# A new order for all pieces of a hand-ordered graph kernel, with one product step cut in two

## Chip, cores and metric

The kernel runs on one core of a Trainium2 chip. The metric is device microseconds (us) of one execution. Times inside an execution come from one profiled run and are counted from the first instruction. TensorE is PE in the profile (PEld is its weight load), VectorE is DVE, ScalarE is ACT, GpSimd is POOL, and SP issues the DMAs.

## What is computed

There are 128 graphs of 128 nodes with 64 features. Layer 0 sums, over each node's neighbours, the positive part of a sum of two projections, and multiplies by a second weight. Layer 1 is a small message pass with a gated update. Each layer ends with a residual and a layer norm.

```python
mask = adj > 0                                            # layer 0
diff = x[:, :, None, :] - x[:, None, :, :]
h = relu((x @ W1a)[:, :, None, :] + diff @ W1b + b1)      # 192 hidden columns
x = layernorm(x + einsum('bjkh,bjk->bjh', h, mask) @ W2 + deg[..., None] * b2)

m = relu(relu(x @ W1 + b1) @ W2 + b2)                     # layer 1
msg = relu(adj @ m)
r, z, n = gates(msg @ W_ih.T + b_ih, x @ W_hh.T + b_hh)
x = layernorm(x + (1 - z) * n + z * x)
```

## The kernel before

The graphs are taken in 32 groups of four. The sparse sum of layer 0 is done with gathers: a 0/1 matrix (`pick0`, `pick1`) picks neighbour rows on TensorE, its product lands in a PSUM tile `pv` that ScalarE has seeded (`seed0`, `seed1`), and ScalarE (`keep`, L656) or VectorE (`reduce`, `reduce1`, L666) takes the positive part and adds it up. There are 24 gather steps of 12 products in a group (L636).

Each group's work is a set of Python generators, one for each kind of piece; each `yield` ends a step, and nearly each step holds the instructions of one engine. The order is written out by hand: `TIMETABLE` gives every step of a kind a number, in units of which 100000 (`PER`) lie between one group and the next. Group g's step is put at g x 100000 plus its number, all steps are sorted, and the program is issued in that order. The numbers are used for nothing else. Every engine works through its own instructions strictly in the order that comes out. `FIRST` replaces the numbers of some kinds for the first group and `SETUP` places the steps of the set-up. The steps of up to six groups lie within one period.

Below, `sums0.1` is the second step (counted from 0) of the kind `sums0`. The steps that the text speaks of:

- `pieces`: step 0 projects x (L547, PE). Steps 1, 2, 5, 6, 9, 10 are ScalarE copies to bf16 (L574) of the two halves; steps 3, 4, 7, 8 subtract each copy in PSUM with one product of 384 columns (L577, PE).
- `sums0`, `sums2`: the turned sums. Step 0 is three transposes (L711, PE). Step 1 is two products of all 128 columns (L718) and two products of 64 columns (L723), four weight loads each because they are float32. The last step copies them to SBUF (L729, ACT).
- `second`: step 0 and 1 are products (L284, L288, PE), step 2 adds a residual and takes the statistics (L292, L254, L256, DVE), step 3 is three tiny GpSimd operations (`ve` L259, `nm` L261, `rs` L263), step 4 one more (L265, `nm` times `rs`), step 5 is four ScalarE operations that write x1 (L269). `turn.0` (L299, PE) transposes x1.
- `update`: step 0 is a tanh (ACT, L361), steps 1 to 4 are GpSimd (L364, L367, L370, L373), step 5 the second statistics (L254, L256, DVE), step 6 `ve`, `nm`, `rs` and step 7 their product on GpSimd, step 8 writes the output (ACT).
- `pick0` (L518 twice, L532 twice) and `pick1` (L518, L540): VectorE compares and subtracts bf16 tiles that all lie in SBUF.
- `offsets`: products (L455), two small copies (L458, L460, ACT), step 2 is four GpSimd operations (L466, `till`), step 3 a product (L469), step 4 two copies (L472, L474).
- GpSimd also has `masks` (L415), `counts`, `others` (L479, L481), `together0` to `together3` (three steps each: L686, L688, L691) and `joined0`, `joined2` (L699). ScalarE also has `base0` to `base3` (L678), `turned.1` (L490), `owners.1` (L498).

PSUM gives three tiles to `pv` and two to everything else, in turn.

Of the kernel before, what the change touches and what calls it, by code (L numbers as in the profile page):

```python
# [28 lines left out]

PER = 100000  # L30
TIMETABLE = {
    "load": (-268618,), "masks": (-266066,), "ranks": (-232900, -232900), "degrees": (-257102, -254423),
    "turned": (-224742, -220574), "counts": (-234901,), "offsets": (-217678, -211964, -197704, -192380, -189932),
    "owners": (-35894, -35894), "places": (-179586, -177714),
    "pieces": (-221915, -212465, -212465, -212025, -212025, -210034, -207896, -206287, -204509, -201502, -201502),
    "others": (-93885, -63613), "values0": (-168677, -168312, -168312), "pick0": (-187243, -177588, -157318, -147219),
    "pick1": (-101562, -99096), "over0": (-86465, -86465), "over2": (-91716, -89070), "base0": (-71690,),
    "base1": (-115079,), "base2": (-74898,), "base3": (-66289,), "together0": (-90368, -86071, -54801),
    "sums0": (-16639, -16639, -6895), "joined0": (-42043,), "joined2": (-9054,),
    "together1": (-31159, -22707, -22707), "together2": (-54332, -29252, -26680), "sums2": (-10324, -7550, -6743),  # L40
    "together3": (-14410, -11697, -11388), "second": (1322, 1729, 6614, 12070, 12714, 14947), "turn": (17589, 19125),
    "message1": (22148, 22871), "message2": (24221, 25357), "message3": (34134, 47496),
    "gates": (52002, 52335, 59212, 59212, 60471, 61641),
    "update": (63484, 134926, 134926, 146356, 147450, 212137, 231447, 236648, 276814),
    "seed0": (-137838, -111380, -107532, -90909, -89996, -88760, -70167, -48540),
    "gather0": (-132826, -123102, -109699, -102053, -101463, -95122, -90696, -82750, -82750, -77811, -77618, -69952,
        -66122, -48012, -38905, -32104), "keep0": (-129922, -97944, -81962, -65602),
    "reduce": (-116740, -102949, -100299, -89511, -89215, -81357, -75312, -71801, -69013, -44762, -33692, -24596),
    "seed1": (-80653, -43141), "gather1": (-77673, -72671, -67801, -55447, -41338, -33923, -28108, -20295),
    "keep1": (-76545, -38998), "reduce1": (-70927, -59829, -52180, -31003, -23063, -16037),  # L50
}


SETUP = (-227883, -212853, -185033, -155144, -101231, 22249)
FIRST = {
    "load": (-236749, -176840), "masks": (-192323,), "ranks": (-160512, -153527), "degrees": (-172354, -159518),
    "turned": (-108605, -102394), "counts": (-146837,), "offsets": (-115482, -109556, -106790, -103472, -99536),
    "places": (-98687, -93949),
    "pieces": (-169807, -166786, -164278, -164278, -164278, -164278, -158634, -152826, -143767, -142875, -113691),
    "values0": (-148521, -139633, -130220), "pick0": (-141784, -133982, -133982, -103074), "pick1": (-92485, -74065),  # L60
    "over0": (-88306, -87641),
}


# [1 line left out]
def adj_resnorm_kernel(  # L66
# [166 lines left out]
    def made(s, key, pool, shape, dtype, **how):  # L233

        if key not in s:
            s[key] = pool.tile(shape, dtype, **how)
        return s[key]
# [146 lines left out]
    with ExitStack() as fast:  # L384
# [259 lines left out]
        def kept(s, t, i):  # L644
            if t:
                return s["acc1", i]
            return s["acc0", i // 2][:, i % 2]
# [56 lines left out]
        def sums(s, i0):  # L704

            def part():
                g, q = s["g"], i0 // 2
                p = ps_w.tile([N, 3, N], F32, tag="w", name=f"ph{g}")
                fs = s["fs", q].rearrange("p b h -> p (b h)")
                for i, c in ((0, 0), (1, 2), (2, 1)):  # L710
                    nc.tensor.matmul(  # L711
                        p[:, i, :], fs[:, c * N : (c + 1) * N], ident, start=i == 0, stop=False, is_transpose=True,
                        skip_group_check=True,
                    )
                yield
                a = kept(s, 1, q)
                for i in range(2):
                    nc.tensor.matmul(  # L718
                        p[:, i, :], a[:, 0, i, i * F : i * F + N], s["ownT"][:, i0 + i, :], start=False, stop=True,
                        skip_group_check=True,  # L720
                    )
                for i in range(2):
                    nc.tensor.matmul(  # L723
                        p[i * F : (i + 1) * F, 2, :], a[:, 0, i, (1 - i) * N : (1 - i) * N + F], s["ownT"][:, i0 + i, :],
                        start=False, stop=True, skip_group_check=True,
                    )
                yield
                hmT = made(s, "hmT", main, [N, 2, 3, N], F32, tag="hmT", name=f"hmT{g}", bufs=2)
                nc.scalar.copy(hmT[:, q], p)  # L729

            return part
# [14 lines left out]
        name, g, run = "setup", -1, setup(ps_g, ps_w)  # L746
        for t in SETUP:
            plan.setdefault(t, []).append(run)
# [143 lines left out]
```

## Time and profile before

| | us |
|---|---|
| median of three runs | 966.61 (966.36 to 968.12) |
| the profiled execution, whole | 966.97 |
| its span, first to last instruction | 965.2 |
| start of the first gather of group 0 | 18.18 |
| of group 2 | 85.73 |
| of group 31 | 906.70 |
| from there to the end | 58.50 |

The span is 1.8 us shorter than the execution. The first two periods take 31.76 and 35.79 us; from group 2 on a period takes 28.29 us nearly without change. The granted clock is 0.98 over the span: the trace has it at 0.5 from 19.4 to 43.3 and from 84.2 to 91.1, and at 1.0 in between and after, up to the end of the program. PE is busy for 907.4 us, DVE 827.3, ACT 841.4, POOL 840.7.

### The profile page before, as it was taken

To read this page: it belongs to the slowest core of one execution; us is meant where nothing else is said; L and a number is where in the kernel's file an instruction comes from. 1 tells how busy PE (TensorE), PEld (TensorE's weight loads), DVE (VectorE), ACT (ScalarE), POOL (GpSimd) and SP (SyncE) were. 2 spreads that over 40 slices of the span, in tenths; PEclk is the share of its full clock that TensorE was granted. 3 is DMA by queue.
4 is the path that set the end of the run, shared out by engine and by line. 5 is a ranking of instruction groups with operands and counts; after the bars stand their busy time and mean duration, and the time that the engine had idled before them with its cause. 6 is when DMAs were issued, how large, how long until landed. Compare 5 with 4: busy or idle time off the path is not lost.

```text
span 965.2 us, 32667 instructions
## 1 busy us (share of the span) xinstructions
PE 907.4 (94%) x13333; PEld 723.1 (75%) x13335; DVE 827.3 (86%) x1586; ACT 841.4 (87%) x1762; POOL 840.7 (87%) x1233
## 2 busy tenths in 40 slices
PE   6888999999999999999999999999999999999984
PEld 3567777777877777878777787777778777777762
DVE  5687898888899888889988888988888898888962
ACT  3787899999999999999999999999999999999863
POOL 4576899999999999999999999999999999999774
PEclk6898999999999999999999999999999999999998
DMA  3000001111100111110001111011101001010000
GB/s 97 24 3 23 24 2 29 30 29 30 29 18 13 30 30 29 30 30 10 22 29 30 30 30 29 2 30 30 30 29 29 25 7 30 29 30 8 7 7 19
DMA packets 25565, 23.91 MB, mean 25 GB/s; under 512 B 4156, under 2 KB 21314, under 8 KB 25410
## 3 DMA queue, kind: packets, MB, share of 16 engines
q1 hardware_dynamic: 25410, 21.78, 7.9%
q8 instruction: 106, 1.74, 0.8%
q14 instruction: 49, 0.40, 0.1%
HBM read 17.57 MB, written 4.19 MB: 23 GB/s over the span
## 4 chain that ended last, share of the span: by engine, by line
PE 68%; ACT 14%; DVE 13%; issue 3%; POOL 1%; DMA 0%; SPq 0%; ACTq 0%; DVEq 0%; POOLq 0%
PE pv L636 32%; DVE acc L666 7%; ACT x L269 4%; PE ph L718 3%; PE pw L284 3%; PE pv L577 3%; ACT pv L606 3%; DVE pick L532 3%; ACT us L623 2%; PE pv L547 2%; PE pu L547 2%; PE ph L723 2%; PE ph L711 2%; PE pm L307 2%; PE pa L327 2%
## 5 line engine op out<-in xcount | busy, mean ns | idle before, releaser
L666 DVE SCALAR_TENSOR_TENSOR acc<-pv,acc 128x768 f32<-128x768 f32 x576 | 534.4, 952 | 102.6 <-PE pv L636 90.4
L636 PE MATMUL pv<-b,pick 64*128 64x192 bf16 x9216 | 465.9, 245 | 21.0 <-DVE acc L666 17.0
L636 PEld LDWEIGHTS <-pick 64*128 64x128 bf16 x9216 | 379.2, 95 | 92.9 <-issue 69.9
L606 ACT COPY pv<-u 128x768 f32<-128x768 f32 x256 | 206.3, 816 | 1.1 <-DVE acc L666 1.0
L656 ACT ACTIVATE acc<-pv 128x768 f32<-128x768 f32 x192 | 155.9, 812 | 17.1 <-PE pv L636 16.9
L686 POOL TENSOR_TENSOR acc<-acc 128x384 f32<-128x384 f32 x128 | 143.7, 1123 | 12.9 <-DVE acc L666 12.9
L466 POOL TENSOR_SCALAR till<-iota,off 128x128 bf16<-128x128 bf16 x128 | 100.3, 801 | 7.8 <-ACT off L458 7.8
L574 ACT CAST b<-pv 128x384 bf16<-128x384 f32 x192 | 83.0, 486 | 19.7 <-PE pv L547 10.5
L691 POOL TENSOR_TENSOR fs<-acc,nb 128x192 f32<-128x192 f32 x128 | 75.9, 593 | 21.6 <-ACT nb L678 14.1
L699 POOL TENSOR_TENSOR acc<-acc 128x384 f32<-128x384 f32 x64 | 77.8, 1216 | 7.3 <-DVE acc L666 7.2
L688 POOL TENSOR_TENSOR acc<-acc 128x192 f32<-128x192 f32 x128 | 77.9, 608 | 2.6
L518 DVE TENSOR_TENSOR pick<-rankT,ramp 128x2048 bf16<-128x2048 bf16 x64 | 77.2, 1208 | 0.7 <-POOL npad L448 0.7
L606 ACT COPY pv<-us 128x768 f32<-128x768 f32 x64 | 51.4, 803 | 26.4 <-DVE acc L666 26.4
L259 POOL TENSOR_SCALAR ve<-mv 128x4 f32<-128x4 f32 x64 | 39.5, 617 | 35.5 <-DVE mv L256 35.4
L263 POOL TENSOR_TENSOR rs<-ve,nhalf 128x4 f32<-128x4 f32 x64 | 66.8, 1043 | 0.0
L415 POOL TENSOR_SCALAR maskT<-adjT 128x512 bf16<-128x512 f32 x32 | 61.2, 1912 | 6.1 <-DMA adjT<-in_adjT_dram 6.0
L617 PE MATMUL pz<-u,own 128*128 128x192 f32 x256 | 57.7, 348 | 0.9 <-ACT own L474 0.9
L678 ACT ACTIVATE nb<-u,npad 128x192 f32<-128x192 f32 x128 | 58.5, 458 | 0.0
L532 DVE TENSOR_TENSOR pick<-pick 128x1024 bf16<-128x1024 bf16 x64 | 50.4, 787 | 0.0
L269 ACT ACTIVATE x<-y,nm,rs 128x64 f32<-128x64 f32 x128 | 45.9, 432 | 4.8 <-POOL nm L265 4.8
L269 ACT ACTIVATE o<-y,nm,rs 128x64 f32<-128x64 f32 x128 | 45.9, 446 | 2.2 <-POOL nm L265 2.2
L617 PEld LDWEIGHTS pz<-u,own 128*128 128x128 f32 x256 | 39.8, 189 | 9.3 <-ACT own L474 5.9
(148 smaller groups left out, 1635.6 us busy)
## 6 DMA issues: line engine op xcount, KB each, us to landing
adjT<-in_adjT_dram SPq DMA_DIRECT2D x32, 256.0 KB, 3.0
xT<-in_xT_dram SPq DMA_DIRECT2D x64, 64.0 KB, 2.7
x<-in_x_dram SPq DMA_DIRECT2D x32, 128.0 KB, 2.3
out_dram<-o SPq DMA_DIRECT2D x32, 128.0 KB, 1.7
wab<-in_w_dram SPq DMA_DIRECT2D x2, 96.0 KB, 2.9
bi<-in_b_ih_dram SPq DMA_DIRECT2D x1, 96.0 KB
bias<-in_b_hh_dram SPq DMA_DIRECT2D x1, 96.0 KB
wx<-in_w_hhT_dram SPq DMA_DIRECT2D x2, 48.0 KB, 2.7
```

Of the source, the lines that this page charges most:

```text
L269: nc.scalar.activation(s[into][:, i, :], y[:, i, :], AF.Identity, bias=nm[:, i : i + 1], scale=rs[:, i : i + 1])
L466: nc.gpsimd.tensor_scalar(s["till"][:, i, :], iota, off[:, i : i + 1], None, ALU.is_lt)
L532: nc.vector.tensor_tensor(v[:, q, 1], v[:, q, 1], v[:, q, 0], ALU.subtract)
L574: nc.scalar.copy(b[c][:, h::2, :], ps[h])
L606: nc.scalar.copy(v, src.to_broadcast(list(v.shape)))
L617: nc.tensor.matmul(p[:, i, :], s["own32"][:, i0 + i, :], s["u"][:, i0 + i, :], start=True, stop=True)
L636: nc.tensor.matmul(v[:, h, j, :], pick[ks], s[f"b{c}"][ks, gr, :], start=False, stop=c == 2, skip_group_check=True,)
L656: nc.scalar.activation(kept(s, t, i), view(s["pv", t, i, 0]), AF.Relu)
L666: nc.vector.scalar_tensor_tensor(out=a, in0=view(s["pv", t, i, k // CH if t == 0 else 0]), scalar=0.0, in1=a, op0=ALU.max, op1=ALU.add,)
L686: nc.gpsimd.tensor_tensor(f[:, 0], f[:, 0], f[:, 1], ALU.add)
L688: nc.gpsimd.tensor_tensor(f[:, 0, 0], f[:, 0, 0], f[:, 0, 1], ALU.add)
L699: nc.gpsimd.tensor_tensor(f[:, 0], f[:, 0], f[:, 1], ALU.add)
```

## The change

One `yield` is added: the two products of 64 columns (L723) become a step of their own, `sums0.2` and `sums2.2`, and the copy to SBUF becomes step 3. All numbers of `TIMETABLE`, `SETUP` and `FIRST` are replaced. No instruction is added, removed or changed; the order in which the engines get them is.

```diff
-    "others": (-93885, -63613), "values0": (-168677, -168312, -168312), "pick0": (-187243, -177588, -157318, -147219),
+    "others": (-118434, -58619), "values0": (-174541, -170553, -168136),
...
-    "together0": (-90368, -86071, -54801),
-    "sums0": (-16639, -16639, -6895), "joined0": (-42043,), "joined2": (-9054,),
+    "together0": (-95088, -76907, -44507), "sums0": (-19812, -13451, -11960, -10058), "joined0": (-34125,),
+    "joined2": (-10568,),
...
-    "update": (63484, 134926, 134926, 146356, 147450, 212137, 231447, 236648, 276814),
+    "update": (62463, 117060, 142675, 149215, 150755, 189123, 200159, 250387, 280080),
...
                         p[:, i, :], a[:, 0, i, i * F : i * F + N], s["ownT"][:, i0 + i, :], start=False, stop=True,
                         skip_group_check=True,
                     )
+                yield
                 for i in range(2):
                     nc.tensor.matmul(
                         p[i * F : (i + 1) * F, 2, :], a[:, 0, i, (1 - i) * N : (1 - i) * N + F], s["ownT"][:, i0 + i, :],
```

Sorting both timetables gives the order on each engine. In a period of the steady part these stretches differ, and nothing else:

```text
PE    before  offsets.0 sums0.0 sums0.1(L718,L723) pieces.3 pieces.4 sums2.0 gather0.2 sums2.1(L718,L723) pieces.7 pieces.8 gather0.3
      after   offsets.0 sums0.0 sums0.1(L718) pieces.3 sums2.0 pieces.4 sums0.2(L723) gather0.2 pieces.7 sums2.1(L718) pieces.8 sums2.2(L723) gather0.3
DVE   before  reduce1.5 reduce.1 pick1.0 reduce.2 pick1.1 second.2 reduce.3 reduce.4 update.5 pick0.0
      after   reduce1.5 update.5 reduce.1 pick1.0 reduce.2 pick1.1 second.2 reduce.3 reduce.4 pick0.0
POOL  before  together3 joined2 offsets.2 others.0 together0.0 second.3 second.4 together0.1 update.6 masks update.1 update.2 others.1
              update.7 together0.2 together2.0 update.3 update.4 joined0 counts together1.0 together2.1 together2.2 together1.1 together1.2
      after   together3 others.0 joined2 offsets.2 update.6 together0.0 second.3 second.4 update.1 together0.1 masks others.1 update.2
              update.3 update.7 update.4 together0.2 together2 together1.0 counts together1.1 together1.2 joined0
ACT   before  update.0 owners.1 ... update.8 turned.1 base1 pieces.1 pieces.2 offsets.1 ... sums0.2 sums2.2 pieces.9 pieces.10
      after   owners.1 update.0 ... turned.1 update.8 pieces.1 offsets.1 pieces.2 ... sums0.3 pieces.9 sums2.3 pieces.10
      before  keep1.0 base2 message2.1 base0 seed0.6 values0.1 values0.2 base3
      after   base2 keep1.0 message2.1 seed0.6 base3 base1 values0.1 base0 values0.2
```

In the first periods, `ranks` of group 0 comes before its `pieces`, `pieces.8` before `values0.0`, and `offsets.0` to `offsets.3` of group 0 come earlier.

## The prediction

> **What bounds the kernel now.** I first read the busy shares and the chain that ended last, then the busy time of the steady part, then the timelines of POOL, DVE and PE's weight loads inside one period.
>
> ```profile
> PE 907.4 (94%) x13333; PEld 723.1 (75%) x13335; DVE 827.3 (86%) x1586; ACT 841.4 (87%) x1762; POOL 840.7 (87%) x1233
> ...
> PE 68%; ACT 14%; DVE 13%; issue 3%; POOL 1%; DMA 0%; SPq 0%; ACTq 0%; DVEq 0%; POOLq 0%
> ```
>
> PE is nearly full, but a third of the chain runs through other engines. The three stretches below (columns: stretch, its length, busy time of PE, PEld, DVE, ACT, POOL, clock, DMA share, GB/s) are the 29 periods from group 2 to group 31, what lies ahead of them, and what lies behind.
>
> ```profile
> 85.80:906.70 820.90, 802.15 (x12058) 645.62 (x12060) 734.83 (x1383) 754.44 (x1586) 761.29 (x1092) 1.00 0.08 24
> 0.00:85.80 85.80, 65.80 (x779) 48.28 (x782) 60.29 (x115) 55.28 (x107) 45.89 (x87) 0.82 0.15 41
> 906.70:965.20 58.50, 39.47 (x503) 29.23 (x500) 32.22 (x91) 31.63 (x71) 33.55 (x56) 0.93 0.04 14
> ```
>
> 820.9 / 29 = 28.3 us a period, so 0.1 us in each period is 2.9 us in the end. Where PE still waits inside a period is seen in its weight loads; the period shown starts at 396.97 (start, length, idle time before and what ended it):
>
> ```profile
> 400.99 0.53 PEld L718 LDWEIGHTS ph<-ownT,acc 128*128 128x128 f32 x4
> 401.63 0.20 PEld L723 LDWEIGHTS ph<-ownT,acc 128*64 128x64 f32 x4
> 402.00 0.11 PEld L577 LDWEIGHTS <-minus 128*128 128x128 bf16 x2 [0.17 <-issue]
> 402.18 0.41 PEld L711 LDWEIGHTS ph<-ident,fs 128*128 128x128 f32 x3
> ...
> 404.80 0.94 PEld L636 LDWEIGHTS <-pick 64*128 64x128 bf16 x24 [0.32 <-issue]
> ...
> 412.51 0.14 PEld L299 LDWEIGHTS pt<-ident,x 128*128 128x128 f32 x1 [0.31 <-ACT x L269]
> ```
>
> Wherever the shape of the weights changes (128*128, 128*64, 64*128), PE loses 0.1 to 0.3 us; between equal shapes (L577 to L711) next to nothing. The last line is the wait that matters most: `turn.0` waits for x1, the end of a chain through `second` on DVE, POOL and ACT. These are POOL and DVE there:
>
> ```profile
> 403.22 3.39 POOL L466 TENSOR_SCALAR till<-iota,off 128x128 bf16<-128x128 bf16 x4
> 406.58 1.27 POOL L479 TENSOR_TENSOR t<-b2bc,deg 128x256 f32<-128x256 f32 x1
> 407.82 0.99 POOL L686 TENSOR_TENSOR acc<-acc 128x384 f32<-128x384 f32 x1
> 409.07 0.23 POOL L259 TENSOR_SCALAR ve<-mv 128x4 f32<-128x4 f32 x1 [0.26 <-DVE mv L256]
> ...
> 410.70 0.20 POOL L265 TENSOR_TENSOR nm<-nm,rs 128x4 f32<-128x4 f32 x1
> ...
> 411.79 1.11 POOL L259 TENSOR_SCALAR ve<-mv 128x4 f32<-128x4 f32 x1 [0.35 <-DVE mv L256]
> ```
>
> ```profile
> 404.42 1.23 DVE L518 TENSOR_TENSOR pick<-place,ramp 128x2048 bf16<-128x2048 bf16 x1
> ...
> 406.44 0.94 DVE L540 TENSOR_TENSOR pick<-pick 128x1536 bf16<-128x1536 bf16 x1
> ...
> 408.90 2.02 DVE L666 SCALAR_TENSOR_TENSOR acc<-pv,acc 128x768 f32<-128x768 f32 x2
> 410.83 0.59 DVE L254 BATCH_NORM_STATS2 stats<-y 128x6 f32<-128x64 f32 x4
> 411.34 0.36 DVE L256 BATCH_NORM_AGGREGATE mv<-stats 128x2 f32<-128x6 f32 x4
> 411.62 1.19 DVE L518 TENSOR_TENSOR pick<-rankT,ramp 128x2048 bf16<-128x2048 bf16 x1
> ```
>
> Two rows of one operation tell the main thing: `ve` of `second.3` took 0.23 us, `ve` of `update.6` 1.11 us. The second was issued at 411.79, while the `pick` of 411.62 ran, and it ended at 412.90, just behind the pick's end at 412.81. A GpSimd operation issued during a pick on DVE stands until the pick is over, however small it is.
>
> **The change, part by part.** Nothing is added, so each engine's sum of work stays; what can change is waiting. Times below are on the shown period.
>
> *PE, turned sums.* From 400.71 to 404.80, 4.09 us, the loads themselves take 2.83 us and the gaps 1.26. After, the shape changes are: L577 to L723 twice, L723 to L636 twice, L636 to L577 once; the others are between equal shapes. L723 to the next is 0.17, L636 to a full array 0.16; L577 to another shape cost 0.32 behind two of the 384-column products, and I take 0.21 behind one. With 0.07 for L711 and L718 behind L577, the gaps are 2 x 0.21 + 2 x 0.17 + 0.16 + 2 x 0.07 = 1.06; the loads are 2.89: four single L577 of 0.10 for two pairs of 0.11, less 0.10 that L711 waited inside its 0.41 (0.31 in the first turned sum) and 0.02 of overlap. Sum 3.95: a gain of 0.14, say 0.15 us (0.35 if L577 to L723 cost nothing, a loss of 0.1 if each cost 0.32). The single products wait for ScalarE's copies: ACT loses `base1` here (0.47) but does `turned.1` first, which waits until PE's L487 are done at about 399.1, so `pieces.1` starts again near 400.8 and its copy is ready at 401.3, ahead of `pieces.3` near 401.5. `offsets.1` before `pieces.2` puts that at 401.8, ahead of `pieces.4` at 402.0. Cover of 0.2 each; without it PE would wait by what is missing.
>
> *DVE.* `update.5` (0.87 from 410.83 to 411.70) moves into the 1.81 us in which DVE waits ahead of `reduce.1` at 403.54; its input was written by POOL nine microseconds before. It costs nothing there, with 0.9 of cover. `pick0.0` then follows `reduce.4` directly, at 410.83 in place of 411.62, less the 0.15 that PE gained: **410.68 to 411.87**. `reduce.5` and `seed1.0` come earlier, which takes PE's wait for `seed1.0` (0.05 to 0.1, taken as 0.08).
>
> *POOL.* Now `update.6` (0.23 + 0.23 + 1.04 with its gaps: 1.55) stands ahead of `together0.0` and `second.3`, and `others.0` has left that place for one ahead of `joined2`. From the end of `reduce.11` at 399.14 POOL runs `together3` (1.01, 0.59, 0.59 and 0.15 between them) from 399.23 to 401.57 (before, it started at 399.94, behind other work), `others.0` to 402.14 (0.61 where no pick stands against it; the 1.27 shown holds a block), `joined2` to 403.10, `offsets.2` from 403.08. Its fourth operation meets `pick1.0` (404.42 to 405.65) and ends 0.46 behind that, at 406.1. `ve` and `nm` get through to 406.6; `rs` is due at 406.58, in `pick1.1` (406.44 to 407.38), and ends about 0.9 behind it, at 408.28 (blocked rows end their own length less 0.14 behind the pick: 412.90, and 406.58 + 1.27). `together0.0` ends at 409.2 and `second.3` starts at 409.2 (409.07 before; between 408.9, where the data would set it, and 409.4, if `nm` is blocked too). The distance from there to `second.4` is 410.70 - 409.07 = 1.63: due at **410.8**. That is inside the moved `pick0.0`.
>
> *What it costs.* `second.4` then ends behind the pick like the blocked `ve`, at 411.87 + 0.09 = 411.96 in place of 410.90. x1 started on ACT at 411.02, now at 412.05; `turn.0` at 413.54 for 412.51. That is 1.03 us of PE standing, and all of PE queues behind `turn.0`: `places`, `message1` and the gathers. The 0.15 gained ahead of it is lost in the same wait. From `turn.0` to the next `gather0.15`, which through `reduce.11` starts POOL's row again, the order on PE is unchanged, so only the 0.08 comes off: **+0.95 us a period** (0.85 to 1.1).
>
> *The rule.* The Trainium skill, "SBUF — State Buffer", section "SBUF: two separate sides", speaks against this move: a VectorE operation of that kind and a GpSimd one take a shared port pair as an exclusive lock for the whole instruction, and the other blocks. The rows agree on the side of GpSimd. By the page a GpSimd operation that came first would hold up DVE just as long; then `pick0.0` would start behind `rs`, and the loss would be some 0.1 us a period larger. The trace has a pick of 1.22 us at 413.60, begun while `rs` of 413.17 ran its 1.04, so I take no hold-up.
>
> *Everything else.* `masks`, `update.1` to `update.4`, `counts`, `joined0` and `base0` to `base3` feed nothing on PE for over 4 us; cover is lost only if POOL is over 0.7 us late at `together3`. SP issues the loads some 13 us ahead of `masks` (400.48 against 414.19), so moved loads and stores cost nothing. The head: before, `gather0.0` of group 0 waits for `pieces.8`, two copies and a seed until 18.18; with `values0.0` behind `pieces.8` I expect about 1 us less, and `offsets` of group 0 earlier perhaps 2 more, since POOL waits 7.8 us for it. I take -3 us (from -6 to +2, the 23.9 us at clock 0.5 there may move). Tail: no next `pick0.0` exists there, 0 +- 1.
>
> *Sum.* 966.97 + 29 x 0.95 - 3 = 991.5 for the profiled execution, which stood 0.36 above the median: **991 us**; with 0.85 to 1.1 and the head's bounds, 984 to 1001.
>
> **The rivals.** *POOL slips through (faster).* `second.4` is due only about 0.1 us inside the pick. If `rs` of `update.6` starts before `pick1.1` (0.14 earlier than I have it), `second.3` is set by its data, 0.15 earlier than before, and `second.4` ends before `pick0.0`. Then a period gains 0.15 + 0.08 = 0.23: 966.6 - 6.7 - 3 = 957. For: PE's switches are really fewer, and the blocks are decided by tenths. Against: `update.6` puts 1.55 us where 0.61 stood. It decides from `second.4` due before about 410.7.
>
> *One block only (about the same).* `rs` is blocked but `second.4` slips in: x1 is 0.13 late, 0.08 comes off, +0.05 a period: 966.6 + 1.5 - 3 = 965.
>
> *In turns.* `till` took 3.39 us in the shown period and 3.09 in others; if the block strikes in half of the periods, 966.6 + 14 - 3 = 977.
>
> *Worse.* POOL, late at `together3` too, holds up the sums: over 1001.
>
> **How the numbers follow.** Blocked in each period 0.55, slips through 0.20, one block 0.12, in turns 0.08, worse 0.05. The likeliest gives 991; its own range is 984 to 1001. To hold 8 in 10 the range must reach to the faster cases: 957 to 1001. A measurement of this kernel tells about 0.2% (1.9 us) from no change. Faster takes slipping through and part of one block: 0.25; same the most of one block: 0.07; slower the rest: 0.68.
>
> **What would show it.** In the changed profile: L265 at `second.4` at about 1 us in place of 0.20, once a period, and the wait of L299 for ACT `x` up from 0.3 to over 1 us; a period of 29.2 us; L577 standing alone with a gap of about 0.2 ahead of L723; no 1.81 us wait of DVE ahead of `reduce.1`. The prediction is wrong if L265 stays at 0.2 us, if the period falls below 28.3, or if L723 costs more behind L577 than 0.3 us.

## The result, and the profile after

The changed kernel takes 1002.57 us (median of 4 runs, 999.02 to 1006.38) against 967.07 for the kernel before (4 runs): a ratio of 1.036, 95% interval 1.034 to 1.038. Slower was forecast, at 991 with a range of 957 to 1001; the time lies 1.6 us above that range. The profiled execution took 999.02, the least of the four; its span is 997.2.

The three stretches of the changed profile, cut at the same pieces as before (first gather of group 2, first gather of group 31):

```profile
81.56:936.83 855.27, 803.11 (x12060) 646.57 (x12060) 739.07 (x1383) 757.46 (x1588) 761.63 (x1092) 0.99 0.08 23
0.00:81.56 81.56, 61.38 (x779) 45.73 (x780) 60.91 (x115) 54.66 (x106) 49.14 (x89) 0.90 0.16 43
936.83:997.16 60.33, 40.58 (x503) 29.88 (x500) 32.26 (x91) 31.61 (x71) 33.05 (x54) 0.90 0.04 13
```

The steady part grew by 34.4 us, the head shrank by 4.2 and the tail grew by 1.8; PE's busy time in the steady part is the same within 1 us (803.11 for 802.15), so nearly all of the time is waiting. An ordinary period takes 29.41 us for 28.29. (A correction to the section on the profile before: the two stretches at clock 0.5 given there are 11.4 us late. By the windows of that profile, 8.0 to 32.0 has 0.50 and 72.8 to 79.7 has 0.51; and the end, from 956.9 on, has 0.50 too, where that section says 1.0.)

The period shown from here on starts at 405.12. PE's weight loads in it (start, length, idle time before and what ended it; L724 is the L723 of the kernel before, one line further down for the added `yield`):

```profile
409.59 0.10 PEld L577 LDWEIGHTS <-minus 128*128 128x128 bf16 x1
409.99 0.41 PEld L711 LDWEIGHTS ph<-ident,fs 128*128 128x128 f32 x3 [0.29 <-issue]
410.36 0.10 PEld L577 LDWEIGHTS <-minus 128*128 128x128 bf16 x1
410.72 0.20 PEld L724 LDWEIGHTS ph<-ownT,acc 128*64 128x64 f32 x4 [0.26 <-issue]
...
421.06 0.14 PEld L299 LDWEIGHTS pt<-ident,x 128*128 128x128 f32 x1 [1.06 <-ACT x L269]
421.72 0.14 PEld L299 LDWEIGHTS pt<-ident,x 128*128 128x128 f32 x1 [0.53 <-ACT x L269]
```

The last two lines are the forecast wait: `turn.0` stands for x1, first 1.06 us and then 0.53, where before it was 0.31. The lines above them are a forecast that failed: behind a single L577 PE loses 0.29 and 0.26 us. GpSimd and VectorE in the same period:

```profile
414.83 0.95 POOL L261 TENSOR_SCALAR nm<-mv 128x4 f32<-128x4 f32 x1
415.76 1.04 POOL L263 TENSOR_TENSOR rs<-ve,nhalf 128x4 f32<-128x4 f32 x1
...
417.86 0.23 POOL L259 TENSOR_SCALAR ve<-mv 128x4 f32<-128x4 f32 x1
...
419.48 0.73 POOL L265 TENSOR_TENSOR nm<-nm,rs 128x4 f32<-128x4 f32 x1
```

```profile
411.88 0.96 DVE L666 SCALAR_TENSOR_TENSOR acc<-pv,acc 128x768 f32<-128x768 f32 x1 [1.20 <-PE pv L636]
...
414.75 0.95 DVE L540 TENSOR_TENSOR pick<-pick 128x1536 bf16<-128x1536 bf16 x1
...
418.93 1.22 DVE L518 TENSOR_TENSOR pick<-rankT,ramp 128x2048 bf16<-128x2048 bf16 x1
```

Two GpSimd operations stand in a pick. `nm` of `update.6`, 0.23 us when nothing is in its way, took 0.95: it came in `pick1.1` (414.75 to 415.70) and ended behind it. That put `second.3` (the `ve` of 417.86) at 12.74 us of the period, for 12.10 before. So `second.4` (L265) came due at 419.48, in `pick0.0`, and took 0.73 for 0.20.

A second loss comes on top of that wait. Windows around two neighbouring periods, and around a stretch inside the first (the column behind the five engines is the granted clock):

```profile
374.20:405.20 31.00, 29.16 (x419) 23.28 (x420) 25.68 (x50) 26.51 (x57) 26.50 (x39) 0.94 0.09 24
405.20:434.60 29.40, 27.56 (x418) 22.19 (x420) 25.52 (x49) 26.18 (x56) 26.41 (x39) 1.00 0.09 25
391.20:394.60 3.40, 3.40 (x30) 2.44 (x30) 0.46 (x1) 2.67 (x6) 3.32 (x4) 0.53 0.00 0
```

Three periods of the steady part take 30.81 to 30.85 us, 1.4 more than the rest. Each holds one stretch of 3.4 us at half clock, and each stretch starts 0.1 to 0.2 us behind the second wait of a `turn.0` (391.0 behind 390.87, 657.2 behind 656.99, 687.9 behind 687.80). The starts lie whole multiples of 3.41 us apart. Before, the steady part has none.

Cut in slices of 3.41 us that begin where the stretches do, the trace shows what comes ahead of each. The first three rows are the slices directly ahead of the three:

```profile
387.54:390.95 3.41, 1.89 (x28) 1.26 (x28) 3.41 (x4) 2.39 (x7) 3.33 (x6) 1.00 0.01 2
653.78:657.19 3.41, 1.89 (x29) 1.35 (x28) 3.41 (x4) 2.39 (x7) 3.33 (x5) 1.00 0.03 5
684.50:687.91 3.41, 1.89 (x28) 1.28 (x27) 3.41 (x4) 2.39 (x7) 3.33 (x5) 1.00 0.00 0
240.77:244.18 3.41, 1.89 (x28) 1.39 (x28) 3.41 (x4) 2.39 (x7) 3.33 (x5) 1.00 0.00 0
```

In them PE is busy for 1.89 us and idle for 1.52, the most in the steady part: both waits of `turn.0` (0.83 and 0.34 us by PE's own records) and the 0.36 ahead of the gather in front of them lie in one slice. In the other periods a boundary parts them. The last row is one more slice with 1.52, with no stretch behind it, so this much idle time did not always do it.

### The profile page after: what moved, and what is told of

It reads as the page before. It is cut to its first block, busy times and chain, and to the rows that moved or that the text cites. A ratio compares the mean times of both kernels' runs of the same rounds, so it can differ in the third digit from the quotient of the medians.

```text
span 997.2 us, 32606 instructions
## 1 busy us (share of the span) xinstructions
PE 905.1 (91%) x13333; PEld 722.2 (72%) x13335; DVE 832.2 (83%) x1586; ACT 843.7 (85%) x1762; POOL 843.8 (85%) x1233
## 5 line engine op out<-in xcount | busy, mean ns | idle before, releaser
L636 PE MATMUL pv<-b,pick 64*128 64x192 bf16 x9216 | 465.1, 244 | 20.6 <-DVE acc L666 16.3
L636 PEld LDWEIGHTS <-pick 64*128 64x128 bf16 x9216 | 377.4, 95 | 88.4 <-issue 64.9
L691 POOL TENSOR_TENSOR fs<-acc,nb 128x192 f32<-128x192 f32 x128 | 85.8, 670 | 82.9 <-ACT nb L678 75.3
L686 POOL TENSOR_TENSOR acc<-acc 128x384 f32<-128x384 f32 x128 | 144.2, 1127 | 8.6 <-DVE acc L666 8.6
L574 ACT CAST b<-pv 128x384 bf16<-128x384 f32 x192 | 88.9, 481 | 17.2 <-PE pv L577 7.8
L518 DVE TENSOR_TENSOR pick<-rankT,ramp 128x2048 bf16<-128x2048 bf16 x64 | 88.3, 1381 | 0.0
L415 POOL TENSOR_SCALAR maskT<-adjT 128x512 bf16<-128x512 f32 x32 | 76.5, 2391 | 6.2 <-DMA adjT<-in_adjT_dram 6.1
L699 POOL TENSOR_TENSOR acc<-acc 128x384 f32<-128x384 f32 x64 | 63.9, 999 | 0.3 <-DVE acc L666 0.3
L678 ACT ACTIVATE nb<-u,npad 128x192 f32<-128x192 f32 x128 | 54.5, 451 | 0.0
L299 PE MATMUL pt<-ident,x 128*128 128x128 f32 x64 | 21.2, 331 | 35.3 <-ACT x L269 35.0
L577 PE MATMUL pv<-b,minus 128*128 128x384 bf16 x128 | 41.7, 329 | 6.3 <-ACT b L574 3.0
```

The costliest lines, as they stand in the source:

```text
L415: nc.gpsimd.tensor_scalar(s["maskT"], s["adjT"], 0.0, None, ALU.is_gt)
L518: nc.vector.tensor_tensor(s[name][:, rows], s[src].rearrange("p (o g) n -> p o g n", o=1).to_broadcast([N, n, G, N]), ramp[:, first : firs ...
L574: nc.scalar.copy(b[c][:, h::2, :], ps[h])
L636: nc.tensor.matmul(v[:, h, j, :], pick[ks], s[f"b{c}"][ks, gr, :], start=False, stop=c == 2, skip_group_check=True,)
L686: nc.gpsimd.tensor_tensor(f[:, 0], f[:, 0], f[:, 1], ALU.add)
L691: nc.gpsimd.tensor_tensor(fs[:, i % 2], f[:, 0, 0], s["nb", i], ALU.subtract)
```

## The experiments

The theory after the result: VectorE's and GpSimd's moves make the period's loss, by picks and GpSimd steps that meet; the new wait of PE adds the half clock. The main rival: TensorE's or ScalarE's new order holds a loss of its own. A run shares its runs of the kernel before with those of the same call; each ratio is to these. Times "of the period" count from the first gather of group 13.

**1. `update.6` back (changed kernel).**

```diff
-    "update": (62463, 117060, 142675, 149215, 150755, 189123, 200159, 250387, 280080),
+    "update": (62463, 117060, 142675, 149215, 150755, 189123, 230000, 250387, 280080),
```

> The changed kernel with one step moved back: update.6 on GpSimd stands behind together0.1, as before the change; update.5 on VectorE stays at its new early place. If the loss is the chain update.6 -> second.3 -> second.4 blocked by pick0.0: second.3 starts when its statistics are ready (12.05 us into the period), second.4 is due at 13.7, just ahead of pick0.0 at 13.8, L265 of second.4 goes from 0.73 back to 0.20 us, the period from 29.41 to 28.2 to 28.4 us, no stretch at clock 0.5 in the steady part, and the time is 960 to 967 us. If the loss came from the new order on PE or ScalarE instead, the time stays above 990 us.

Measured 974.94, ratio 1.009 (1.007 to 1.010); period 28.69, L265 at 0.20 in every row, no half clock in the steady part. Most of the loss is gone, so the two moves together made it; but 0.40 us of a period stayed, which the theory did not have. Of it 0.33 arises at the turned sums (run 7).

**2. The sums in one step again (on top of 1).**

```diff
-    "sums2": (-12965, -10018, -8883, -5893)
+    "sums2": (-12965, -11320, -11319, -5893)
```

(and `sums0` and `pieces.4` to match.)

> The first kernel of this call (changed kernel, update.6 back) with the order of the turned sums on PE undone: both L718 and L724 products together again, pieces.3 and pieces.4 together, pieces.7 and pieces.8 together; ScalarE's order as changed. By the prediction's sum of gaps the split order gains 0.15 us a period, so this one would be 4 us slower than the first. By the trace of the changed kernel, where gather0.3 starts at 7.85 us of the period against 7.83 before, the split gains nothing: within 1.5 us of the first.

Measured 1040.81, ratio 1.077 (1.075 to 1.079). A failed experiment: the number put `sums2.1` ahead of `joined2`, so its products read the accumulators before their last addition, and `joined2` waited for them in turn. It says nothing of the split.

**3. `update.5` early, alone (kernel before).**

```diff
-    "update": (63484, 134926, 134926, 146356, 147450, 212137, 231447, 236648, 276814),
+    "update": (63484, 134926, 134926, 146356, 147450, 190000, 231447, 236648, 276814),
```

> The kernel before with one step moved: update.5 on VectorE goes from ahead of pick0.0 into VectorE's wait ahead of reduce.1. pick0.0 can then start at 13.86 us of the period, and second.4 is due at 13.73. If the GpSimd step decides (update.6 ahead of second.3), nothing is blocked here: period 28.2 to 28.3 us, time 963 to 967 us. Rival: the move on VectorE alone is enough, since second.4 is only 0.13 us ahead of pick0.0; then L265 is blocked, the period is 29.2 us and the time about 995 us.

Measured 975.97, ratio 1.010 (1.009 to 1.012), between the two expectations; period 28.63, L265 never blocked. GpSimd and VectorE there (the period starts at 398.23):

```profile
412.05 1.65 POOL L688 TENSOR_TENSOR acc<-acc 128x192 f32<-128x192 f32 x1
...
420.67 1.01 POOL L686 TENSOR_TENSOR acc<-acc 128x384 f32<-128x384 f32 x1
```

```profile
412.02 1.22 DVE L518 TENSOR_TENSOR pick<-rankT,ramp 128x2048 bf16<-128x2048 bf16 x1
...
421.06 1.17 DVE L532 TENSOR_TENSOR pick<-pick 128x1024 bf16<-128x1024 bf16 x1
```

The earlier `pick0.0` (412.02 to 413.24) holds `together0.1`: 1.65 us for 0.59. From `update.1` on GpSimd is 0.37 us late, and now it is VectorE that stands: `pick0.2`, due in mid-`together2.0`, ends 0.55 behind that operation's end (420.67 + 1.01) and takes 1.17 for 0.75. Before, it ended 0.56 behind the same operation, which ran 0.34 earlier in the period. The loss of the period is that 0.34.

**4. `update.5`, `update.6` and `others.0` moved together (kernel before).**

```diff
-    "others": (-93885, -63613)   "update": (..., 212137, 231447, ...)
+    "others": (-110500, -63613)  "update": (..., 190000, 205000, ...)
```

(`others` of the first group kept at -93885.)

> The kernel before with three steps moved: update.5 into VectorE's wait ahead of reduce.1, others.0 ahead of joined2, update.6 between offsets.2 and together0.0 on GpSimd; all else as before, PE's and ScalarE's order too. If these moves alone make the loss: second.3 starts at 12.2 to 12.7 us of the period, second.4 is due at 13.8 to 14.3 and blocked by pick0.0 (13.86 to 15.05), the wait of turn.0 grows by 1.0 to 1.1 us, the period is 29.2 to 29.5 us, some stretches of 3.4 us at clock 0.5 appear, and the time is 995 to 1007 us. If the loss needs the rest of the new order, it stays at 965 to 970 us.

Measured 1013.06, ratio 1.049 (1.047 to 1.050): more than the whole loss with TensorE and ScalarE as before. Period 29.82, L265 at 0.60, and two half-clock stretches. Of the 1.53 us in a period 0.48 is a cost of this version: with `others.0` ahead, `joined2` ends at 6.82 of the period and `sums2.1` waits for it. The rest arises at `turn.0`, with the waits of the changed kernel (the period starts at 413.80):

```profile
428.74 0.60 POOL L265 TENSOR_TENSOR nm<-nm,rs 128x4 f32<-128x4 f32 x1
```

```profile
430.20 0.14 PEld L299 LDWEIGHTS pt<-ident,x 128*128 128x128 f32 x1 [1.06 <-ACT x L269]
```

**5. `update.5` and `update.6` back (changed kernel).**

```diff
-    "update": (62463, 117060, 142675, 149215, 150755, 189123, 200159, 250387, 280080),
+    "update": (62463, 117060, 142675, 149215, 150755, 209000, 230000, 250387, 280080),
```

> The changed kernel with two numbers put back: the normalization's statistics (update.5) directly ahead of pick0.0 again, as before, and update.6 (the tiny GpSimd normalization) behind the first two steps of together0, as before. Theory (these two moves carry the whole loss; in the run with update.6 alone put back, the 0.40 us that were left in a period were GpSimd's: the first pick held together0.1, the queue ran late, and the turned sums waited 0.31 us for its last subtraction): the period is back at 28.2 to 28.4 us and the head keeps its 4 us, 960 to 967. Rival (TensorE's new order has a loss of its own of 0.3 us in a period): 970 to 976.

Measured 979.76, ratio 1.014 (1.012 to 1.016); period 28.87. A miss: PE is as before up to `gather0.9`, then +0.40 at `gather0.10` and +0.18 at `gather1.1` (a wait that run 9 has too). `pick0.0`, due at 14.66 as before, ended at 16.25 for 15.84. The change also has `update.1` ahead of `together0.1`; the two held GpSimd from 13.89 to 15.17.

**6. `pick0.0` behind `reduce.5` (changed kernel).**

```diff
-    "pick0": (-189417, -183923, -162136, -156277)
+    "pick0": (-188200, -183923, -162136, -156277)
```

> The changed kernel with one number changed: pick0.0 stands behind reduce.5 instead of ahead of it, so that VectorE waits for gather0.8 when second.4 comes due at 14.35 us of the period, and no pick runs there; update.5 and update.6 stay early. Theory (second.4 lost 0.53 us to pick0.0, and nm lost 0.73 us to pick1.1, one after the other): turn.0 comes 0.53 us earlier, the period is 28.8 to 29.0, and with fewer stretches at half clock the time is 977 to 986. If nm's block is the one that counts, or the later picks push reduce.6 back: 995 or more.

Measured 982.99, ratio 1.017 (1.015 to 1.018), as expected; period 28.89. Here `nm` of `update.6` is blocked as in the changed kernel (0.95), but L265 is not, and PE's first wait is half as long:

```profile
416.72 0.20 POOL L265 TENSOR_TENSOR nm<-nm,rs 128x4 f32<-128x4 f32 x1
```

```profile
417.78 0.14 PEld L299 LDWEIGHTS pt<-ident,x 128*128 128x128 f32 x1 [0.54 <-ACT x L269]
```

The second transpose of `turn.0` starts 1.06 us later in the changed kernel's period than before (16.60 for 15.54), and here 0.53 (16.07). So the 1.06 us are two delays of 0.53, one behind the other. The one that goes away here is L265 in `pick0.0`, shown by this run. The other is `second.3`, 0.64 us late behind `update.6`; that `nm`'s block (0.72 us) makes it is read from the rows, and no run takes that block alone away. With 0.53 gone the half clock is gone from the steady part too, and no 3.41 us slice there holds more than 1.01 us of idle PE.

**7. The split alone (kernel before).** The added `yield`, and TensorE's order of the turned sums as in the changed kernel.

```diff
-    "sums0": (-16639, -16639, -6895)   "sums2": (-10324, -7550, -6743)
+    "sums0": (-16639, -16639, -10200, -6895)   "sums2": (-10324, -7550, -4400, -4300)
```

(and `pieces.4`, `pieces.7` to match.)

> The kernel before with one part of the change: the 64-column products as a piece of their own, in the changed kernel's order on TensorE (pieces.3, first turned sums, pieces.4, 64-column products, gather0.2, pieces.7, 128-column products of the other pair, pieces.8, 64-column products); no other piece moved. By the prediction's count of changes of shape: 0.15 us less in a period, 962 (961 to 964). By the gaps in the changed kernel's trace (0.29 behind the first single product, 0.26 behind each of the others): no gain, 966 to 967.

Measured 975.39, ratio 1.009 (1.008 to 1.011): worse than both expectations, +0.33 us in a period. (PE and GpSimd; the period starts at 398.02.)

```profile
403.40 0.20 PEld L711 LDWEIGHTS ph<-ident,fs 128*128 128x128 f32 x2 [0.42 <-POOL fs L691]
```

```profile
402.75 0.59 POOL L691 TENSOR_TENSOR fs<-acc,nb 128x192 f32<-128x192 f32 x1
```

The transposes now come ahead of a product and meet the last subtraction of `together3`, which ends at 5.33 of the period. Before, the same transpose ran at 5.37, with a product ahead of it, and lost at most 0.05. The same wait is 0.38 us in run 1, where GpSimd is as late; in the changed kernel GpSimd ends it at 4.68.

**8. PE's wait filled (changed kernel).**

```diff
+            for i in range(8):
+                nc.tensor.matmul(p.rearrange("p a b -> p (a b)"), ones_h, zeros[:, 0 : 2 * N], start=True, stop=True)
             for i in range(2):
                 nc.tensor.transpose(p[:, i, :], s["x1"][:, 2 * i : 2 * i + 2, :], ident)
```

> The changed kernel with eight products of 256 columns of zeros into turn's own tile ahead of its two transposes, so that TensorE does not idle through its wait for x1; no step is moved. Theory (the wait of over 1 us is what makes the clock fall to half for single stretches of 3.4 us): no record at half clock in the steady part, the period stays at 29.4, the time is 990 to 997 and the runs lie closer together than 999 to 1006. Rival (the stretches come by themselves): 999 to 1006 as before.

Measured 994.2 (993.74 to 995.99), ratio 1.029 (1.027 to 1.030), as expected. The periods of the steady part take 29.40 to 29.42, all but those at its two ends, and no record there is at half clock; no 3.41 us slice holds more than 0.69 us of idle PE. The products fit into the wait (L299 is here the added products, L301 the transposes):

```profile
420.40 0.77 PEld L299 LDWEIGHTS <-ones_h 128*128 128x128 bf16 x8 [0.16 <-issue]
421.30 0.14 PEld L301 LDWEIGHTS pt<-ident,x 128*128 128x128 f32 x1
```

Work that computes nothing made the kernel some 8 us faster (8.4 by the medians, 7.5 by the ratios to the kernel before).

**9. `update.1` back too (on top of 5).**

```diff
-    "update": (62463, 117060, 142675, 149215, 150755, 209000, 230000, 250387, 280080),
+    "update": (62463, 134926, 142675, 149215, 150755, 209000, 230000, 250387, 280080),
```

> The changed kernel with three numbers put back: update.5 ahead of pick0.0, update.6 behind together0.1, and update.1 (the first GpSimd step of the gated update) behind masks, as before; TensorE's, ScalarE's and the other GpSimd steps stay in the changed order. In the run with the first two alone put back, GpSimd ran update.1 and then together0.1 from 13.89 to 15.17 us of the period, pick0.0 (due at 14.66) ended at 16.25 instead of 15.84, and the 0.41 us went through reduce.5, seed1.0 and gather1.0 into the period. Theory (every loss of the period is a VectorE pick and a GpSimd step that meet): pick0.0 ends at 15.8 again, the period is 28.2 to 28.4 us, the head keeps 4 us, and the time is 959 to 966, below both kernels. Rival (TensorE's or ScalarE's new order holds a loss of its own): a period of 28.6 or more, 972 or more.

Measured 975.28, ratio 1.008 (1.007 to 1.010); period 28.66. `pick0.0` takes 1.19 us again, so that part held. The rest is mainly three small waits: the transposes of run 7 again (+0.18, `together3` ended at 5.18), `gather1.1` (+0.17; `base2` stands ahead of `keep1.0` on ScalarE), and `pick0.2`, which met other GpSimd steps (1.02 for 0.75). The theory missed and the rival's numbers hold: the first of these waits belongs to TensorE's new order, the second to ScalarE's.

**10. `update.1` early, alone (kernel before).**

```diff
-    "update": (63484, 134926, 134926, 146356, 147450, 212137, 231447, 236648, 276814),
+    "update": (63484, 113000, 134926, 146356, 147450, 212137, 231447, 236648, 276814),
```

> The kernel before with one number changed: update.1 on GpSimd ahead of together0.1, directly behind second.4, instead of behind masks; nothing else moves. Theory (a pick that comes due while a GpSimd step runs waits until that step has ended): update.1 runs from 13.9 to 14.65, together0.1 starts at 14.6, just ahead of pick0.0's 14.65, and holds it to 15.2; pick0.0 ends 0.4 us later and the period is 0.4 to 0.6 us longer, 977 to 984. Rival (a GpSimd step costs VectorE nothing, only the reverse): the time of before, 966.

Measured 977.16, ratio 1.011 (1.009 to 1.013), as expected; period 28.69. GpSimd and VectorE (the period starts at 400.85):

```profile
415.42 0.59 POOL L688 TENSOR_TENSOR acc<-acc 128x192 f32<-128x192 f32 x1
```

```profile
415.50 1.60 DVE L518 TENSOR_TENSOR pick<-rankT,ramp 128x2048 bf16<-128x2048 bf16 x1
```

The pick came 0.08 us behind a GpSimd step of 0.59 and ended 1.09 behind its end: 1.60 for 1.19. So a pick is held by a step like this one too, if that comes first.

**11. The orders of before, with the change's head (changed kernel).** GpSimd's, VectorE's and TensorE's steps of a period put back into exactly their old order, and `base2` behind `keep1.0`.

```diff
-    "others": (-118434, -58619)   "joined0": (-34125,)   "together1": (-39808, -38898, -36490)
+    "others": (-104000, -58619)   "joined0": (-41500,)   "together1": (-39400, -38898, -36490)
-    "update": (62463, 117060, 142675, 149215, 150755, 189123, 200159, 250387, 280080),
+    "update": (62463, 134926, 141000, 156000, 156100, 209000, 230000, 250387, 280080),
```

(and `base2`, `pieces`, `sums0`, `sums2`, `together2`.)

> The changed kernel with numbers put back until GpSimd, VectorE and TensorE run a period in exactly the order of before (the 64-column products again directly behind their 128-column products, update.1 to update.6, others.0, joined0, together1 and together2 in their old places) and base2 behind keep1.0 on ScalarE; ScalarE keeps the other small exchanges of the change, and the head, the set-up and the first group keep the changed order. Theory (the period's loss is the order of GpSimd, VectorE and the turned sums; the head's gain is apart from it): a period of 28.25 to 28.4 us, the head 2 to 4 us shorter, 961 to 967 and at or below before. Rival (ScalarE's exchanges or the change's head cost the difference): 970 or more.

Measured 986.29, ratio 1.020 (1.019 to 1.022); period 29.02. A miss, and the rival holds. GpSimd:

```profile
421.79 0.60 POOL L691 TENSOR_TENSOR fs<-acc,nb 128x192 f32<-128x192 f32 x1 [0.84 <-ACT nb L678]
```

`together0.2` needs `base0`, which ScalarE still did late (its end was 22.99 of the period, for 20.25). The change had moved both; putting one back left the other waiting.

**12. `base0` back too (on top of 11).**

```diff
-    "base0": (-68304,)   "base1": (-72399,)    "base3": (-74898,)
+    "base0": (-77000,)   "base1": (-115079,)   "base3": (-66289,)
```

(and `seed0.6`, `values0`.)

> The kernel of the run with the orders of before (GpSimd, VectorE and TensorE as before, the change's head), with base0, base1, base3, seed0.6 and values0 back in their old places on ScalarE too. In that run GpSimd's subtraction in together0.2 stood from 22.23 to 23.07 us of the period waiting for base0, which ScalarE did at 22.99 instead of 20.25; the queue behind it ran 0.7 us late and the turned sums waited for together3's last step. Theory (that one wait was the whole 0.73 us of its period): a period of 28.25 to 28.4 us with the head 2 to 5 us shorter, 960 to 966, below before. Rival (something else of the change holds the loss): 975 or more.

Measured 968.7 (11 runs), ratio 1.0016 (1.0006 to 1.0025); period 28.46. That is above the 960 to 966 expected. Nearly all of the loss went, but 0.16 us stayed: `update.8` of 1.44 us ahead of `pieces.1`, and `offsets.1` ahead of `pieces.2`, made `pieces.4` late.

**13. ScalarE's last three exchanges back (on top of 12).**

```diff
-    "offsets": (-221550, -213750, ...)   "update": (62463, ..., 280080)
+    "offsets": (-221550, -213200, ...)   "update": (61000, ..., 274000)
```

> As the run with base0 back, and three more steps of ScalarE in their old order: offsets.1 behind pieces.2, update.8 ahead of turned.1, update.0 ahead of owners.1. Every engine now runs a period in the order of before; the head, the set-up and the first group keep the change's order. In the run with base0 back update.8 (1.44 us) stood directly ahead of base1 and pieces.1, pieces.2 ended at 5.16 instead of 4.63 us of the period, and pieces.4 on TensorE waited 0.16 us for it. Theory (that is the last of the period's loss, and the head's gain of 3 to 4 us is apart from it): a period of 28.3 us and 963 to 965, faster than before by 0.2 to 0.4%. Rival (the head's gain is given back at the end or in the first periods): 966 to 968.

Measured 963.95 (962.17 to 964.70), ratio 0.996 (0.9945 to 0.997), as expected: faster than both kernels. Its steady part is that of before to 0.2 us:

```profile
81.03:902.10 821.07, 802.14 (x12058) 645.90 (x12059) 734.97 (x1383) 751.40 (x1588) 761.71 (x1092) 1.00 0.08 24
```

In the profiles the head is 4.7 us shorter than before and the end 1.4 longer; the medians of the call differ by 3.9. So the change's order outside the steady part is a gain by itself. The 4.7 is not all order: in that head the profile of before is at half clock for 30.7 us, this one for 17.1. Run 3 (old head) and this run have their clock up at the same time (22.2 and 22.1) and reach group 2 at 83.60 and 81.03, 2.6 us apart, run 3 with 3.4 us more at half clock on the way.

## Why the prediction was wrong, and what of it held

*The mechanism held.* `second.4` came due inside the moved `pick0.0`, x1 came late, and PE stood in front of `turn.0` with everything else behind it: +1.06 us at its second transpose, forecast 1.03. Run 4 (only VectorE's and GpSimd's steps moved) and run 6 (only the meeting in `pick0.0` taken away) show it; run 3 shows that `update.5` by itself does not do it. The one rival above 1001 is not what happened: it had GpSimd late at `together3`, which ended at 4.68 of the period, for 5.32 before.

*GpSimd's row: right sum, other parts.* The blocked operation of `update.6` was `nm`, not `rs`. By the row's own times `nm` was due 0.02 us ahead of `pick1.1` (406.1 and 0.32 behind it, against 406.44); it left out the 0.08 us that the changed profile has between `till` and `ve`. `rs` then ran its 1.04 us behind `nm`, and `second.3` started at 12.74 of the period, where the row had 12.2, or 12.4 with `nm` blocked. So `second.4` came due 0.53 us later than forecast, nearer to the pick's end, and its block cost 0.53 us where the sum gave it 0.96 (410.8 to 411.96, less 0.20). The sum came out all the same, as the end of `pick0.0` sets the end of `second.4` wherever in the pick it comes due. Run 6 parts the two delays: 0.53 and 0.53.

*`update.5`.* Its 0.87 us cost VectorE nothing in its new place, as forecast: the wait ahead of `reduce.1` fell from 1.81 to 1.20.

*TensorE's 0.15 us did not come.* This term was mis-sized: the gap of L711 behind L577 was taken as 0.07 and was 0.29, and the two of the 64-column products were 0.26 for 0.21. So the reading that gaps go with a change of shape fails: L577 and L711 are both 128*128 and lost 0.29. (The bound of 0.35 for products that follow at no cost is a slip; that sum gives 0.14 + 2 x 0.21 = 0.56.) The forecast itself gave the 0.15 up in the wait of `turn.0`, so this did not move it. `gather0.3` starts at 7.85 of the period for 7.83. Run 7 shows a price that the step lacked: the split order needs `together3` earlier.

*After `turn.0`.* The 0.08 us expected from an earlier `seed1.0` did not last; by the end of the period the segment is 0.06 longer. With the term before, the period came to +1.12 for +0.95. Over 29 periods, less 0.9 for three longer periods of before that have no counterpart, and 1.4 because the first two are less slow, that is about 30 us (34.4 less 4.3 for the clock gives 30.1) for 27.6.

*The step that failed: the sum had no price for PE's wait beyond the wait.* It let the clock move in the head alone and put it at nothing in the steady part, without a reason. Three half-clock stretches of 1.4 us make the other 4.3 us of the steady part in the profile. Run 8 fills the wait, keeps the period at 29.41 and comes to 994.2, inside the range. So by the medians the missing term is some 8 us, more than the three stretches, which were counted in the fastest of the four runs. The 2.5 us by which the period's term was too small would not by themselves have left the range.

*Head and tail.* The head, -4.2 for -3, was inside its bounds, in part by luck: it is at half clock for 17.1 us, before for 30.7, and how much of the 4.2 is order was not parted. The tail grew 1.8 where 0 +- 1 was given. It holds a stretch of 3.4 us at half clock (from 978.0) that the tail of before lacks, but the wait ahead of it is no new one (2.52 us; 2.59 before), and in run 8 the tail grew by 1.4 without such a stretch.

*The rule.* The forecast took no hold-up of VectorE by GpSimd, from one row: a pick begun while `rs` ran. For `rs` that was right again (418.93, 1.22 us, while an `rs` ran to 419.40). For GpSimd's larger operations (`together`, `update.1`) it was wrong: runs 3, 5 and 10 show picks that end 0.34 to 0.41 us late behind a step that had begun first. That is what the Trainium skill, "SBUF — State Buffer", section "SBUF: two separate sides", says of the shared port pair; the page makes no exception for an operation like `rs`, and the traces show one. In the changed kernel itself `pick0.0` met only `rs`, so this did not move the forecast; `pick0.1` was held there (1.59 us for 1.22, behind `together0.1`), but VectorE then waited 1.57 us for PE in any case. The hold-up makes the loss of runs 3 and 10 and 0.40 of the 0.58 us in run 5.

*The clock.* The same skill, "TensorE: Matmul & The Clock Gate", section "Why this matters for your kernels", asks for no idle gap of PE over about 3 us. Here 1.06 and 0.53 us of waiting, with one transpose between them, halved the clock in three of 29 periods; with 0.54 and 0.52 (run 6) it did not happen in the steady part. So shorter waits were enough here than the page's rule names. The page's section "What's actually happening" describes a free-running activity window of about 3.4 us, and the starts at whole multiples of 3.41 us agree with it.

What stays open: the stretches were counted in one profile, and that they make the spread of the changed kernel's runs (999 to 1006) is argued only from the smaller spread of run 8 (993.7 to 996.0). The mean clocks of the four runs (0.980, 0.977, 0.975, 0.982, in the order 999.02, 1006.38, 1002.67, 1002.47) do not settle it. How much idle time lowers the clock is open too: in run 2 a slice with 1.11 us of it has a stretch at half clock behind it, and most with 1.55 have none. Nor was it tried which of the first group's moves makes the head's gain, or what lengthens the end.

## What to carry to other kernels

In a schedule written out by hand, look at pairs, not at queues: a VectorE operation on bf16 in SBUF and a GpSimd step that overlap can hold up the one that comes second until the first is done, and a cover of 0.17 us (run 10) ahead of such a meeting is soon gone. Moves that belong together (a step and what it waits for on another engine) have to be made and undone together; here versions with the same work lay between 964 and 1013 us. A wait of TensorE, here of 1.06 us and 0.53 more, is paid twice where it lowers the clock, and idle products were then worth their place.

## What the runs showed that was not expected

- TensorE's clock fell to half for one stretch of 3.4 us, at 1.4 us each, after waits of 1.06 and 0.53 us, in 3 of 29 periods. Ahead of each lay 3.41 us with 1.52 of idle PE, the most of the steady part (a fourth such slice had no effect). Eight products of zeros in that wait (0.77 us of weight loads) removed it.
- A VectorE pick is held by a GpSimd addition that began first (1.60 for 1.19 us behind a step of 0.59), but not by an `rs` of 128x4 that takes 1.04.
- One product of L577 alone cost 0.29 us ahead of L711 and 0.26 ahead of L724, and nothing ahead of L718; the pair had cost 0.07 ahead of L711 and 0.32 ahead of L636. Splitting the pair bought nothing (7.85 us of the period for 7.83).
